# A four-layer graph network: its own order of work for the first and last three graphs, two layers in other layers' buffers, a new order for the graphs between

## The chip, the cores and the metric

The kernel runs on one core of one Trainium2 chip. The metric is the device time of one execution in microseconds (us); less is better. The core has TensorE (PE in the profile, its weight loads PEld), VectorE (DVE), ScalarE (ACT), GpSimd (POOL) and SyncE (SP), which run their own streams of instructions and wait for each other by semaphores.

## The reference

Thirty-two independent graphs, each with 512 nodes of 256 features (`x`) and a 512x512 adjacency matrix of 0 and 1 (`adj`). Each graph goes through four layers; every layer normalizes, takes the positive part, and adds its result to `x`:

```python
    h = jnp.maximum(_layernorm(x, axis=-1), 0.0)
    x = x + _L0_gnn_ref(h, adj, L0_gnn_W, L0_gnn_a_src, L0_gnn_a_dst)
    h = jnp.maximum(_layernorm(x, axis=-1), 0.0)
    x = x + _L1_gnn_ref(h, adj, L1_gnn_W, L1_gnn_a)
    h = jnp.maximum(_layernorm(x, axis=-1), 0.0)
    x = x + _L2_gnn_ref(h, adj, L2_gnn_a_0, L2_gnn_a_1, L2_gnn_a_2, L2_gnn_a_3)
    h = jnp.maximum(_layernorm(x, axis=-1), 0.0)
    x = x + _L3_gnn_ref(h, adj, L3_gnn_Wqkv, ...)
```

Layer 0 is graph attention with 4 heads: `Wh = h @ W`, scores from a sum of a source and a destination term, masked softmax, product with `Wh`, elu. Layer 1 is the same with one head and a softmax over the other axis. Layer 2 scores pairs of nodes by weighted inner products of `h`, softmax, product with `h`. Layer 3 is a transformer block with 8 heads of 32: qkv, masked softmax attention, output product, layer norm, two products with 1024 features between, layer norm.

## The kernel before

**The work of a graph.** `quick_path` writes every graph as 497 jobs, each for one engine (a job of PE is one to eight products of f32). I name a job by its number in the graph, `#0` to `#496`, which is its place in the table too:

| jobs | what |
|---|---|
| #0, #1 | loads of `adj` and `x` (SP) |
| #2 to #13 | masks `m`, `mT` (four transposing DMAs, #4 to #7) and `m3`; #3 checks `adj` |
| #14 to #42 | layer 0: norm, `h0`, its transposes on PE (#33 to #41) |
| #43 to #66 | layer 0: `wh` (PE #43 to #59), `ps_sp` (#63), and the trip of `rows` through DRAM (SP #65, #66) |
| #67 to #109 | layer 0: four heads (DVE `p`, PE `ps_o` #71 to #74, #81 to #84, #91 to #94, #101 to #104), elu and sum (#107 to #109) |
| #112 to #185 | layer 1: norm, transposes (#131 to #139), `wh` (#141 to #151), `ps_sp` (#156), trip of `rows` (#158, #159), `mc` and `p` (DVE #160 to #174), product `ps_o` (PE #176 to #182) |
| #189 to #264 | layer 2: norm, transposes (#208 to #216), scores (#220 to #252), product `ps_o` (PE #253 to #262) |
| #267 to #371 | layer 3: norm, transposes, qk and v, attention (`ps_s`, `ps_ct`, `ps_to`) |
| #373 to #414 | layer 3: `ps_wo` (#373 to #380), norm (#381 to #404), transposes `ps_t` (#405 to #412) |
| #417 to #496 | layer 3: `ps_f` (#417 to #438 and #441 to #473), last norm, store |

**The order.** Nothing is ordered by loops at run time. `Plan.put` (line 150) gives each job a place, `number * ROUND + table[at]` with ROUND = 100000 (line 153), and `carry_out` (line 178) emits all jobs of all graphs sorted by place, so each engine gets its stream in that order and works it off strictly in order. One table, `PLACES` (line 282), serves all 32 graphs. It runs from 0 to 491,710, so five graphs are in work at a time, one round apart.

**Buffers.** `K` (line 351) lists the kinds of buffers and their slots. Layer 0 has one slot each of `h0`, `h0T`, `wh0`, `rows0`, `e0`, and six of `p`. Layers 1 and 2 share `h1`, `h1T`, `wh1`, `p1`. Layer 3 has `h3`, `hT3`, `qk`, `vt`, `n` and two slots of `p3`. PSUM has two slots of `ps_a`, two of `ps_b`, and `ps_ct`, `ps_to`. A job that is first to use a slot waits for all users of the tile that was there.

**Constants.** The weights of layer 3 are loaded by POOL after the first `x` (line 795), and a few constants are formed at place 150000 (line 798), with one product `ps_bv`.

All of the jobs' instructions are made in `carry_out`, so the profile puts nearly all of DVE's and ACT's work at L214, PE's products at L259 and transposes at L257, DMAs at L235; tiles tell them apart.

Of the kernel before, what the change touches and what calls it, by code (L numbers as in the profile page):

```python
# [16 lines left out]
OP = mybir.AluOpType  # L17
AX = mybir.AxisListType

P = 128  # L20
# [102 lines left out]
class Plan:  # L123
# [6 lines left out]
        tensor_copy=(1,), tensor_scalar_max=(1,), tensor_scalar_mul=(1,),  # L130
    )

    def __init__(self, tc, table):
        self.tc, self.nc, self.table = tc, tc.nc, table
        self.jobs = []

    def graph(self, number):

# [11 lines left out]
    def put(self, engine, takes, ends, outs, ins, call, port=False, moves=None):  # L150

        j = Job()
        place = self.number * ROUND + self.table[self.at] if self.place is None else self.place
        j.place = (place, self.at)
        self.at += 1
        j.engine, j.takes, j.ends, j.call, j.port, j.moves = engine, takes, ends, call, port, moves
        j.after, j.homes = [], []
        before = set()
        for part, writes in [(p, True) for p in outs] + [(p, False) for p in ins]:
            h = part.home  # L160
            r0, r1 = int(part.rows.min()), int(part.rows.max())
            i0, i1 = int(part.index.min()), int(part.index.max())
            if in_psum(part):
                i0, i1 = 0, 1 << 20
            for k, w, a0, a1, b0, b1 in h.uses:
                if (w or writes) and k is not j and a0 <= r1 and r0 <= a1 and b0 <= i1 and i0 <= b1:
                    before.add(k)
            h.uses.append((j, writes, r0, r1, i0, i1))
            if h not in j.homes:
                j.homes.append(h)  # L170
                h.left += 1
        for k in before:
            assert k.place < j.place, "out of order"
            k.after.append(j)
        self.jobs.append(j)
        return j
# [61 lines left out]
    def load(self, tile, source, behind):  # L238
# [7 lines left out]

        return self.put("POOL", 1.0, 0.1, [], [], call)

    def matmuls(self, takes, *calls):

        real = lambda x: x.real() if isinstance(x, Part) else x

        def call():
            made = []
            for c in calls:
                if len(c) == 3:
                    made.append(self.nc.tensor.transpose(*map(real, c)))  # L257
                else:
                    made.append(self.nc.tensor.matmul(*map(real, c[:3]), start=c[3], stop=c[4]))  # L259
            return made  # L260

        outs = [c[0] for c in calls]
        ins = [x for c in calls for x in c[1:3] if isinstance(x, Part)]
        return self.put("PE", takes, takes + 0.2, outs, ins, call)
# [10 lines left out]
def width(args):  # L275
# [4 lines left out]

ROUND = 100000
PLACES = [
    19807, 0, 43241, 57619, 64598, 73580, 81389, 88138, 134062, 235662, 143142, 287307, 285553, 232853, 15635,
    15811, 28841, 27985, 23993, 15811, 30374, 30229, 32369, 32370, 32370, 32446, 32844, 48496, 34324, 44230,
    44177, 46695, 46041, 50344, 54161, 54792, 54792, 54792, 51041, 51777, 57310, 57310, 57310, 57738, 57738,
    57832, 57739, 58104, 61341, 61341, 67966, 61898, 61898, 67567, 69254, 72469, 69482, 77323, 74000, 76325,
    79818, 78024, 78024, 80713, 80713, 80714, 82170, 88138, 93984, 93675, 88138, 100363, 101562, 103520,
    103520, 103520, 103520, 99026, 98456, 107942, 108892, 114155, 115978, 115979, 116955, 117229, 118109,
    112967, 112266, 118498, 118106, 122333, 124077, 124856, 124856, 126720, 126720, 130323, 126361, 126793,
    124647, 132760, 132760, 132760, 132760, 134221, 134221, 134221, 134221, 134221, 134727, 134221, 156322,  # L290
    140191, 134912, 142057, 169073, 157725, 170057, 172384, 201862, 202787, 205641, 207797, 208539, 176096,
    208573, 211867, 216328, 218484, 218484, 219056, 219056, 219056, 219056, 219056, 218484, 218484, 218484,
    218484, 218485, 227052, 227119, 228253, 219613, 219613, 220424, 224906, 224906, 228631, 223683, 224122,
    224122, 229201, 229201, 232797, 231582, 232020, 232794, 233389, 243904, 244480, 249048, 254893, 242125,
    242231, 243790, 254173, 237217, 238008, 241105, 245079, 237839, 238826, 242604, 256707, 257566, 258334,
    259006, 259006, 259006, 259519, 259519, 259519, 259519, 259519, 392456, 255868, 267182, 259006, 259006,
    259892, 259665, 259006, 259006, 259892, 259665, 266786, 266786, 268621, 269711, 273176, 302934, 273176,
    273176, 273176, 277010, 277447, 281097, 281097, 281195, 281196, 281196, 281682, 281682, 281682, 281682,
    281683, 281196, 281683, 282840, 282840, 284327, 283254, 286775, 286821, 286821, 287236, 288036, 287335,
    282681, 282681, 283122, 282681, 284575, 293213, 293213, 295654, 291792, 291574, 293905, 297714, 297584,  # L300
    297714, 298819, 298819, 297714, 287489, 287489, 290592, 290231, 298206, 300033, 308229, 310297, 310297,
    303799, 303799, 303799, 305379, 305380, 306132, 308300, 312883, 316207, 394029, 437737, 327509, 328548,
    327753, 325228, 328998, 329876, 332238, 330645, 332238, 332502, 332502, 332608, 332717, 364575, 332717,
    332717, 332717, 332717, 332717, 338203, 340406, 340406, 340406, 340407, 340407, 340905, 341309, 341309,
    352943, 347109, 352371, 352371, 353369, 353369, 353417, 354661, 356381, 356381, 356381, 357144, 357399,
    346769, 348254, 348493, 351248, 352029, 352189, 352199, 352199, 352554, 359237, 359237, 359237, 359237,
    364034, 360298, 360301, 360448, 365688, 377452, 366095, 368722, 368232, 374829, 379739, 379671, 380891,
    379672, 382370, 383191, 386847, 392755, 392755, 387818, 392756, 395158, 396303, 407857, 382331, 382331,
    382615, 382634, 388690, 385894, 388773, 389314, 389314, 394131, 390806, 394842, 396200, 401293, 405927,
    398693, 403322, 398865, 403593, 407530, 409955, 410479, 412422, 412422, 408793, 409986, 423530, 354795,  # L310
    408893, 410479, 418263, 418263, 418263, 419191, 419191, 419191, 419191, 419128, 417119, 437177, 437347,
    419191, 420203, 420203, 420203, 420203, 420721, 420203, 420203, 421199, 422452, 422452, 423633, 423633,
    432009, 424134, 424134, 424718, 424718, 424759, 425616, 425916, 425916, 425916, 425916, 426698, 426841,
    426841, 426970, 427475, 430939, 430939, 427202, 428368, 428368, 428368, 429763, 429360, 431209, 431243,
    432263, 432263, 432291, 432540, 430070, 430071, 430071, 430071, 430446, 430071, 431829, 432836, 432836,
    435307, 436332, 440746, 435945, 435945, 436252, 436626, 436626, 437927, 444318, 444318, 444811, 444811,
    444811, 445291, 445291, 445291, 445291, 445447, 445572, 436110, 437653, 437653, 437653, 437653, 437653,
    438770, 440843, 440843, 440843, 440843, 440843, 440872, 442233, 442446, 442446, 442446, 445600, 445600,
    442446, 442446, 445601, 445601, 442446, 442704, 446845, 449648, 449758, 449759, 449759, 454221, 449777,
    450699, 450699, 450699, 450699, 450699, 450699, 491710,  # L320
]


# [1 line left out]
def quick_path(  # L325
# [35 lines left out]
    K |= {tag: Kind(dram, tag, 2) for tag in ("rows0d", "rows1d", "to_d", "in_d")}  # L361
    K |= {"ps_ct": Kind(psum, "ps_ct", 1), "ps_to": Kind(psum, "ps_to", 1)}
    K |= {"ps_a": Kind(psum, "ps_a", 2), "ps_b": Kind(psum, "ps_b", 2)}
    plan = Plan(tc, PLACES)

    def new(tag, name, shape, dtype=F32):
        return plan.tile(K[tag], name, shape, dtype)


    ident = const.tile([P, P], F32, name="ident")  # L370
# [295 lines left out]
    def layer3(b, x_t, m3):  # L666
# [29 lines left out]
        for g in range(KD):  # L696
            ps_ct = new("ps_ct", "ps_ct", [P, N])
            ps_to = new("ps_to", "ps_to", [P, N])
            for j in range(NT):
# [8 lines left out]
                        for r, at in enumerate(heads)  # L708
                    ),
                )  # L710
                p = new("p3", "p3", [P, HG, N])
                for q in range(HG // 2):
                    plan.act("activation", p[:, 2 * q : 2 * q + 2], ps[q], AF.Exp)
                plan.dve("tensor_mul", p, p, m3[:, j : j + 1].flat(lambda t: t.to_broadcast([P, HG, N])))
# [53 lines left out]
        for g in range(NF // 2):  # L768
            ps = new("ps_b", "ps_f1", [P, 2, N])
            if g % 2 == 0:  # L770
                f1 += [new("p3", f"f1_{b}", [P, HG, N])] * 4
            for q in (0, 1):
                f = 2 * g + q
                for k in range(KD):
                    plan.matmuls(FULL, (ps[:, q], ff1_t[:, k, cut(f, P)], tT[:, k], k == 0, k == KD - 1))
            for q in (0, 1):
                f = 2 * g + q
                plan.act("activation", f1[f][:, f % 4], ps[:, q], AF.Relu, bias=ff1b_c[:, f : f + 1], fixed=0.27)
# [13 lines left out]
        plan.dma(out[b].rearrange("(t p) d -> p t d", p=P), y, 1.75)  # L792


    plan.aside(max(PLACES[:2]) + 1)
    for tile_, source in late:
        plan.load(tile_, source, lambda: first)
    plan.aside(ROUND + ROUND // 2)
# [518 lines left out]
```

## Time and profile before

| | us |
|---|---|
| median of 3 runs (3751.09 to 3758.95) | 3752.26 |
| the profiled execution: its time | 3758.1 |
| the profiled execution: its span, first to last instruction | 3756.2 |

| | busy us | share of the span |
|---|---|---|
| PE | 3635.0 | 97% |
| PEld | 2366.4 | 63% |
| DVE | 2732.6 | 73% |
| ACT | 1803.8 | 48% |

The mean granted clock of TensorE is 0.976. The profiled execution's span is within 2 us of its own time, and its time is 5.8 us above the median. The page's slices are 94 us each; the start and the end of the span need finer windows.

### The profile page before, as it was taken

To read this page: it belongs to the slowest core of one execution; us is meant where nothing else is said; L and a number is where in the kernel's file an instruction comes from. 1 tells how busy PE (TensorE), PEld (TensorE's weight loads), DVE (VectorE), ACT (ScalarE), POOL (GpSimd) and SP (SyncE) were. 2 spreads that over 40 slices of the span, in tenths; PEclk is the share of its full clock that TensorE was granted. 3 is DMA by queue.
4 is the path that set the end of the run, shared out by engine and by line. 5 is a ranking of instruction groups with operands and counts; after the bars stand their busy time and mean duration, and the time that the engine had idled before them with its cause. 6 is when DMAs were issued, how large, how long until landed. Compare 5 with 4: busy or idle time off the path is not lost.

```text
span 3756.2 us, 51774 instructions
## 1 busy us (share of the span) xinstructions
PE 3635.0 (97%) x19974; PEld 2366.4 (63%) x19974; DVE 2732.6 (73%) x6267; ACT 1803.8 (48%) x3393; POOL 11.1 (0%) x25
## 2 busy tenths in 40 slices
PE   4799999999999999999999999999999999999996
PEld 4666766666766666666666666666666666666553
DVE  4577777877777777777787777787777777777653
ACT  1245445555444555444555544555544455544543
POOL 1000000000000000000000000000000000000000
PEclk7599999999999999999999999999999999999998
DMA  4111111111111111011111111111111111100000
GB/s 120 57 32 33 36 49 46 43 42 36 29 49 46 43 49 36 23 47 47 49 43 38 40 29 49 46 43 49 29 29 49 46 43 49 38 29 27 15 9 11
DMA packets 152349, 152.72 MB, mean 41 GB/s; under 512 B 87840, under 2 KB 122144, under 8 KB 148000
## 3 DMA queue, kind: packets, MB, share of 16 engines
q1 hardware_dynamic: 149632, 144.35, 13.8%
q0 software_dynamic: 1216, 3.94, 0.3%
q8 instruction: 159, 2.61, 0.3%
q10 hardware_dynamic: 1248, 1.05, 0.1%
q14 instruction: 94, 0.77, 0.1%
HBM read 114.57 MB, written 17.96 MB: 35 GB/s over the span
## 4 chain that ended last, share of the span: by engine, by line
PE 95%; DVE 3%; ACT 1%; DMA 1%; issue 1%; SPq 0%; ACTq 0%; DVEq 0%
PE ps_o L259 25%; PE ps_f L259 24%; PE ps_s L259 7%; PE ps_ct L259 7%; PE ps_wh L259 6%; PE ps_qk L259 6%; PE ps_to L259 6%; PE ps_e L259 4%; PE ps_t L257 4%; PE ps_v L259 3%; PE ps_wo L259 3%; DVE p L214 1%; PE ps_y L257 1%; DVE st L214 0%; DMA mT<-m 0%
## 5 line engine op out<-in xcount | busy, mean ns | idle before, releaser
L259 PE MATMUL ps_o<-wh,p 128*128 128x65 f32 (+1 forms) x5120 | 750.5, 303 | 30.2 <-DVE p L214 24.6
L259 PEld LDWEIGHTS ps_o<-wh,p 128*128 128x128 f32 x5120 | 705.6, 200 | 102.7 <-issue 60.5
L214 DVE TENSOR_TENSOR p<-p,m 128x2048 f32<-128x2048 f32 x256 | 582.7, 2286 | 29.7 <-ACT p L214 29.6
L214 ACT ACTIVATE p<-ps_s 128x1024 f32<-128x1024 f32 x512 | 501.2, 1022 | 208.1 <-PE ps_s L259 205.3
L259 PE MATMUL ps_f<-tT,ff_t 128*128 128x512 f32 x1024 | 462.7, 602 | 1.7 <-ACT tT L214 1.7
L259 PE MATMUL ps_f<-ff_t,f 128*128 128x256 f32 x2048 | 461.0, 379 | 0.0
L259 PEld LDWEIGHTS ps_f<-ff_t,f 128*128 128x128 f32 x2048 | 381.9, 190 | 64.0 <-issue 15.3
L214 DVE SCALAR_TENSOR_TENSOR p<-rows,rt,mT 128x512 f32<-128x512 f32 x512 | 370.1, 735 | 16.7 <-DMA mT<-m 16.7
L214 ACT ACTIVATE h<-x,shift,rstd 128x256 f32<-128x256 f32 x512 | 268.6, 595 | 152.8 <-PE ps_o L259 106.3
L259 PEld LDWEIGHTS ps_f<-tT,ff_t 128*128 128x128 f32 x1024 | 189.4, 192 | 229.3 <-issue 188.7
L259 PE MATMUL ps_s<-qk 32*128 32x512 f32 x2048 | 294.2, 640 | 1.3 <-ACT qk L214 0.8
L259 PE MATMUL ps_ct<-p,v 128*32 128x512 f32 x2048 | 272.0, 603 | 9.3 <-DVE p L214 6.3
L214 ACT ACTIVATE f<-ps_f,ff1b_c 128x512 f32<-128x512 f32 x256 | 164.8, 682 | 235.7 <-PE ps_f L259 235.7
L259 PE MATMUL ps_to<-p,ones 128*32 128x512 f32 x2048 | 266.6, 592 | 0.0
L259 PE MATMUL ps_qk<-h3T,wqkv_t 128*128 128x512 f32 x512 | 239.1, 594 | 0.0
L259 PE MATMUL ps_o<-h,p 128*128 128x257 f32 x1024 | 239.0, 385 | 0.0
L259 PEld LDWEIGHTS ps_o<-h,p 128*128 128x128 f32 x1024 | 190.1, 191 | 51.5 <-issue 26.0
L214 DVE BATCH_NORM_STATS2 st<-x 128x6 f32<-128x256 f32 x512 | 195.6, 415 | 6.8 <-DMA x<-in_x_dram 4.7
L214 ACT ACTIVATE rstd<-mv,eps 128x4 f32<-128x4 f32 x192 | 56.4, 294 | 298.6 <-DVE mv L214 286.0
L257 PE MATMUL ps_t<-ident,h 128*128 128x128 f32 x1024 | 172.6, 281 | 25.0 <-ACT h L214 17.6
L259 PEld LDWEIGHTS ps_s<-qk 32*128 32x128 f32 x2048 | 81.3, 182 | 164.6 <-ACT y L214 78.0
L257 PEld LDWEIGHTS ps_t<-ident,h 128*128 128x128 f32 x1024 | 130.8, 145 | 85.2 <-issue 52.3
(131 smaller groups left out, 4322.9 us busy)
## 6 DMA issues: line engine op xcount, KB each, us to landing
adj<-in_adj_dram SPq DMA_DIRECT2D x32, 1024.0 KB
rows<-rows_d SPq DMA_DIRECT2D x32, 1024.0 KB
x<-in_x_dram SPq DMA_DIRECT2D x32, 512.0 KB
rows<-rows_d SPq DMA_DIRECT2D x32, 512.0 KB
out_dram<-y SPq DMA_DIRECT2D x32, 512.0 KB
inv<-in_d SPq DMA_DIRECT2D x32, 256.0 KB
ff_t<-in_L_gnn_W_dram POOLq DMA_DIRECT2D x2, 1024.0 KB, 12.5
mT<-m SPq DMA_TRANSPOSE x128
```

Of the source, the lines that this page charges most:

```text
L214: return [getattr(unit, method)(*map(real, args), **{k: real(v) for k, v in kw.items()})]
L257: made.append(self.nc.tensor.transpose(*map(real, c)))
L259: made.append(self.nc.tensor.matmul(*map(real, c[:3]), start=c[3], stop=c[4]))
```

## The change

It does four things. A graph can have a table of its own (`own`), and the first three graphs (`FIRST`) and the last three (`LAST`) get one each. `PLACES` is replaced, for the 26 graphs between. In graph 1, the layer-0 tiles h0, h0T, wh0, rows0 and e0 lie in layer 3's buffers; in graph 31, layer 3's tiles lie in layer 0's buffers, and its `p3` and `f1` in `p1` and `adj`. A method `accumulate` is added that nothing calls. No job is added or removed: the 497 jobs of a graph, their operations and their sizes stay.

```diff
-    def __init__(self, tc, table):
-        self.tc, self.nc, self.table = tc, tc.nc, table
-        self.jobs = []
+    def __init__(self, tc, table, own=()):
+        self.tc, self.nc, self.table, self.own = tc, tc.nc, table, dict(own)
+        self.jobs, self.number = [], None
...
-        place = self.number * ROUND + self.table[self.at] if self.place is None else self.place
+        place = self.number * ROUND + self.own.get(self.number, self.table)[self.at] if self.place is None else self.place
...
 PLACES = [
-    19807, 0, 43241, 57619, 64598, 73580, 81389, 88138, 134062, 235662, 143142, 287307, 285553, 232853, 15635,
...
-    450699, 450699, 450699, 450699, 450699, 450699, 491710,
+    4941, 0, 45989, 55878, 52736, 53088, 65883, 75806, 126827, 257141, 153885, 318759, 211656, 217633, 19570,
...
+    442345, 444396, 453835, 453835, 478083,
+]
+
+FIRST = [
+    [
+        -232641, -430519, -208468, -143305, -187563, -187562, -126023, -120210, -1386, 231738, 69096, 52945,
...
-    plan = Plan(tc, PLACES)
+    own = {**dict(enumerate(FIRST)), **{B - len(LAST) + g: places for g, places in enumerate(LAST)}}
+    plan = Plan(tc, PLACES, own)
+
+    ELSEWHERE = {
+        1: dict(h0="n", h0T="hT3", wh0="p3", rows0="qk", e0="vt"),
+        B - 1: dict(h3="h0", hT3="h0T", qk="rows0", vt="e0", n="wh0"),
+    }
 
     def new(tag, name, shape, dtype=F32):
+        tag = ELSEWHERE.get(plan.number, {}).get(tag, tag)
         return plan.tile(K[tag], name, shape, dtype)
...
-                p = new("p3", "p3", [P, HG, N])
+                p = new("p3" if b < B - 1 else ("p1", "adj")[j % 2], "p3", [P, HG, N])
...
-                f1 += [new("p3", f"f1_{b}", [P, HG, N])] * 4
+                f1 += [new("p3" if b < B - 1 else ("p1", "adj")[g // 2], f"f1_{b}", [P, HG, N])] * 4
...
-    plan.aside(max(PLACES[:2]) + 1)
+    plan.aside(max(FIRST[0][:2]) + 1)
```

What the tables say is an order, which follows from sorting the places. PE's stream at the start, with g0 for graph 0 and the products' numbers:

| before | after |
|---|---|
| g0 #33 to #59, #63 | g0 #33 to #59, #63 |
| g0 heads #71 to #94 | g0 heads #71 to #94 |
| g0 head #101 to #104 | g1 transposes, with g0 #101 to #104 between |
| `ps_bv` | g1 `wh` #43 to #49, `ps_bv`, g1 `wh` #53 to #59 |
| g1 transposes, `wh`, #63 | g1 #63 |
| g1 #71 to #84 | g1 #71 to #74, half of g0 layer-1 transposes, g1 #81, other half, #82 to #84 |
| g0 layer-1 transposes, `wh` with g1 #91 to #94 between | g0 layer-1 `wh`, #156 |
| g0 #156, g1 #101 to #104 | g1 #91 to #94, g2 transposes, two `wh`, g1 #101 to #104 |
| g2 transposes, g0 #176 to #182 with g2 `wh` between | g0 #176 to #182, six `wh` of g2 |

On SP, the four `mT` transposes of a graph stood on both sides of `rows_d` and `rows` (#65, #6, #66, #7); for g0 and g1 they now all stand ahead of #65. `x` of g1 is loaded right after `adj` of g0, `x` of g2 after `rows` of g0. On DVE, g0's `mc` and `p` of layer 1 (#160 to #174) stood behind g1's elu (#108, #109); most of them now stand ahead of g1's last head. At the end, PE had g31 #253 to #262 in two parts ahead of g30 `ps_wo` and then g30 #405; now g30 `ps_wo` comes first, then three of the four `ps_o` of g31, then g30 #405. From g31's attention on, PE's order is the old one, up to two products of the last `ps_f`.

## Prediction

> **What bounds the kernel now.** I read three views in this order: busy time in windows (columns: the window, its length, then PE, PEld, DVE, ACT, POOL busy with counts, PE's granted clock, DMA share, GB/s), the chain that ended last, and the timeline of the two ends.
>
> ```profile
> 25.00:75.00 50.00, 28.80 (x128) 27.75 (x128) 20.37 (x47) 2.72 (x6) 0.00 (x0) 0.54 0.21 63
> 75.00:125.00 50.00, 33.49 (x135) 28.96 (x135) 18.45 (x48) 8.29 (x22) 0.00 (x0) 0.60 0.21 64
> 125.00:175.00 50.00, 33.66 (x119) 26.32 (x119) 26.27 (x77) 14.41 (x37) 0.00 (x0) 0.60 0.12 33
> 600.00:1600.00 1000.00, 1000.00 (x5601) 650.55 (x5603) 762.42 (x1750) 504.14 (x952) 0.00 (x0) 1.00 0.15 41
> 3600.00:3625.00 25.00, 19.10 (x86) 11.15 (x85) 18.36 (x42) 4.78 (x10) 0.00 (x0) 0.83 0.02 5
> 3675.00:3757.00 82.00, 52.47 (x250) 26.96 (x250) 31.48 (x54) 22.98 (x35) 0.00 (x0) 0.87 0.04 11
> ```
>
> In the middle PE has no idle time and the full clock; no other engine is over 0.77 busy. At the start PE is idle a third of the time and runs at about half its clock. The chain of waits gives the middle's pace:
>
> ```profile
> 303.75 8.84 PE ps_f L259 x20
> 415.13 8.84 PE ps_f L259 x20
> 526.51 8.85 PE ps_f L259 x20
> ```
>
> One graph each 111.38 us, and 32 of them are 3564 us. The span is 3756.2, so 192 us lie outside. To place them I use the first arguments of `matmuls` as the measure of PE work (108.5 us a graph; 111.38 were measured, a factor of 1.026). At 247.1 us PE has begun products with 107.4 us of work ahead of them: 110.2 at the middle's pace, so the start costs **137 us**; the end costs **about 53** and the rest nothing. Only these ends can give much. What they consist of is in PE's timeline (start, us, instruction, idle before it and who ended it):
>
> ```profile
> 34.78 0.66 PE L259 MATMUL ps_o<-wh,p 128*128 128x65 f32 x2 [9.96 <-DVE p L214]
> 36.68 7.52 PE L259 MATMUL ps_o<-wh,p 128*128 128x65 f32 x34 [1.24 <-DVE p L214]
> 62.22 7.06 PE L259 MATMUL ps_o<-wh,p 128*128 128x65 f32 x32 [2.86 <-DVE mv L214]
> 76.55 2.04 PE L259 MATMUL ps_bv<-wo_t,bv_w 128*128 128x256 f32 x4 [7.28 <-issue]
> 95.96 0.66 PE L259 MATMUL ps_o<-wh,p 128*128 128x65 f32 x2 [8.89 <-DVE p L214]
> ...
> 144.11 1.11 PE L257 MATMUL ps_t<-ident,h 128*128 128x128 f32 x4 [5.71 <-DVE mc L214]
> 148.04 1.11 PE L257 MATMUL ps_t<-ident,h 128*128 128x128 f32 x4 [2.82 <-ACT h L214]
> ...
> 3617.57 2.17 PE L257 MATMUL ps_t<-ident,n 128*128 128x128 f32 x8 [5.03 <-ACT n L214]
> 3707.73 2.16 PE L257 MATMUL ps_t<-ident,n 128*128 128x128 f32 x8 [5.03 <-ACT n L214]
> ```
>
> A head's 32 records take 7.1 us in the start. The idle time is graph 0's and graph 1's trips of `rows` (10 and 9 us), graph 0's elu (7), graph 0's layer 1 around 144 us (11 in three pieces), and two norms at the end (5 each).
>
> **What the Trainium skill says.** "Trainium Kernel Development and Optimization", Performance Expectations: matmul busy time is a bad metric since matmuls are pipelined; here it reads 97% while 192 us lie outside the pace, so I don't use it. "TensorE: Matmul & The Clock Gate", part 1 (What's actually happening): the array starts throttled to half its clock, and about 3.4 us of sustained activity releases it. The trace agrees on the two levels (0.50 and 1.00 in windows of 4 us) but not on the release: heads ran 7 us without a gap at 0.50, so heads alone don't warm it. "DMA: Bandwidth & Descriptors" (Two DMAs through the same engine are not ordered): a reader of what another DMA writes must wait for its semaphore; so SP stands still between `rows_d` and `rows`, which took 1.23 us where nothing stood between (132.03 to 133.26).
>
> **The start, step by step.**
> - *Graph 0 up to its heads.* All four `mT` go ahead of `rows_d`. The first `p` waited for the last one, issued at 28.34; it will wait for `rows`, at most 1 to 2 us less. `x` of graph 1 (512 KB) now stands behind `adj` while the DMAs are full (share 0.96 to 1.22): at 382 GB/s up to 1.4 us more. I take 0, bounds -2 and +1.4.
> - *Graph 0's heads* (34.8 to 69.3 us). DVE now does graph 1's `m` (1.22) and `m3` (1.22) between `p`s, so head 1 starts some 2 us later; graph 1's transposes (8 of 0.21) fill the 2.86 before the last head. I take 0, bounds -2 and +3.
> - *Graph 1's layer 0.* Before, its `h0` waited for graph 0's elu (buffer `h0`), and 26.7 us passed from the last head (69.3) to its first (95.96). Now transposes are done by then. What is left: 8 `wh` of 0.9 cold (half before `ps_bv`), `ps_bv`, whose `bv_w` is on DVE behind graph 0's elu (ends near 75), so at about 77; then the other `wh`, `ps_sp` near 82. Then `rows`: 0.3 (spr) + 1.4 + landing. Packets of layer 1's 512 KB ended 3 us after issue; 1 MB gets 4 to 5. First `p` near 88 to 89 in place of 95.06: **-6**. `ps_bv` limits it now. If it came free at once, it would be -9.
> - *Graph 0's layer 1.* DVE stood in order: at 138.44 it turned to graph 1's elu, and `mc` came at 143.43 although `rows` had been issued at 133.26. Now `mc` and `p` (4 x 0.68, 4 x 0.83, small ones) lie under graph 1's last two heads (2 x 7 us cold). From the end of the last head to `ps_o` of layer 1 were 13.5 us (138.4 to 151.9), with only 2 us of transposes; the transposes now come before. So **-11**, and bounds -13 (all) and -6 (if `rows` or `p` is late, as DVE also has graph 1's `p`).
> - *Up to saturation* (161 to 230 us) the order is nearly the same, layer 2 of graph 0 still being a chain of its own; **-1**, bounds -4 and +2. A warm clock is not in the sum: if layer 1's `wh`, now contiguous (3.45 us of work, 7 cold), releases it, the two heads and transposes behind it (about 8.7 us of work) take that much less: up to -8.
>
> Sum of the start: **-18**, bounds -28 and -8.
>
> **The end.** Graph 30's `ps_wo` now has 5.4 us of graph 31's `ps_o` behind it. From the last `ps_ct` (3605.4) to the norm's `ps_t` (3617.6) were 12.2 us with 7.1 of work. After: DVE's two halves of 1/sum (1.76 + 0.42 each) hold `ps_wo` about 1 us, then all is covered; 10.9 of work in about 11.8, so -4. The clock fell in that gap (0.83), and 13.7 us of `ps_f` took 16.9: another -3. Graph 29's same norm had 2.4 us of idle, half of it covered: -1. For graph 31 nothing covers its norm (5.03), attention (some 10 us of gaps) and tail from 3740.8 on, and the order is the old one; the new buffers take waits away that PE doesn't feel there. Sum **-8**, bounds -10 and -3.
>
> **The middle.** PE is full, so only small losses can change. 108.5 against 111.38 is spread over hundreds of jobs; the largest single loss, `ps_wh` to `ps_f` #417, is 0.16. A PE job that needs a new wait on another engine cost 0.034 on average, any other 0.011. Sorting the new table gives 63 such jobs a graph, 65 before: -0.05 us a graph. Following each wait back by data alone with the trace's durations, the tightest has 0.53 us to spare (0.19 before), and 25 have under 2 us (31 before). So **0** over some 27 graphs, bounds -0.3 and +0.4 a graph: -8 and +11.
>
> **Sum.** -18 - 8 + 0 = -26. The profiled execution's own time of 3758.1 would be 3732; the median of the runs, 5.8 lower, becomes **3726 us**.
>
> **Rivals.**
> 1. *The clock warms in the start too* (-8), and the middle gains 0.2 us a graph (-5): 3713. For: at 156 us dense `ps_o` of layer 1 went from 0.60 to 1.00 within 4 us. Against: at 116 to 131 us `wh` mixed with heads stayed at 0.50.
> 2. *The start's gain is given back before saturation*: layer 2 and 3 of graph 0 wait for DVE, now with more of graph 1's and 2's work ahead. Then the end's 8 remain and a little: 3742. Against: DVE is busy 0.4 to 0.6 there.
> 3. *The middle gets slower.* In the old order 11.2 us of PE work lie between layer 1's `ps_sp` and the first `mc` on DVE; in the new one 4.1, and the trip takes 0.3 + 1.2 + 3.2 = 4.7. DVE would stand in front of it with everything queued behind: graph 13's and 15's `p`, norms, whose users on PE have as little as 0.5 us to spare. Graph 1's elu (1.06 ACT, 2 x 1.23 DVE) stands ahead of it and should cover it. It decides above 1 us a graph (26 / 27); at 1.5 it gives 3726 + 41 = 3767.
> 4. *A place is wrong* (a buffer taken too early, a constant used before it is formed): I found graph 0's first `ps_qk` at 326134 behind the constants at 150000; this has no chance worth a number.
>
> **How the numbers follow.** Forecast 0.60 (own range 3709 to 3744), warm start 0.15, given back 0.10, slower middle 0.15. A measurement of this kernel tells 0.2% (7.5 us) from no change. Faster: 0.60 + 0.15 and a third of case 2, less 0.02 of the forecast's upper end: 0.76. Same: 0.09. Slower: 0.15. The range must reach past case 2 but not to case 3: **3704 to 3750**; it leaves out 0.15 above and some 0.04 below.
>
> **What would show it.** Right: graph 1's first head near 89 us, layer 1's `ps_o` within 2 us of graph 1's last head and near 135, no idle above 1 us before `ps_t` near the last-but-one norm, the pace still 111.4. Wrong: a pace above 112, idle time of DVE ended by the DMA `rows` in the middle, or PE not full by 215 us.

## The result, and the profile after

The changed kernel takes 3743.20 us in the median of 12 runs (3737.76 to 3745.93), the kernel before 3755.12 (3750.60 to 3760.10); the ratio is 0.9966, interval [0.9958, 0.9975]. It is faster, by 12 us, inside the predicted range of 3704 to 3750, but by less than half of the 26 us that the prediction worked out. The profiled execution took 3737.76 us with a span of 3735.4, which is 20.8 less than that of before. That is more than the medians differ, and the reason is at the end of this section.

Busy time in windows, changed kernel (columns as in the prediction's first view):

```profile
75.00:125.00 50.00, 35.84 (x150) 29.64 (x149) 26.07 (x68) 8.77 (x27) 0.00 (x0) 0.60 0.21 64
125.00:175.00 50.00, 41.22 (x188) 33.57 (x188) 33.97 (x95) 15.83 (x36) 0.00 (x0) 0.82 0.16 53
175.00:225.00 50.00, 45.83 (x264) 30.72 (x263) 33.59 (x85) 27.25 (x57) 0.00 (x0) 1.00 0.07 19
225.00:275.00 50.00, 47.43 (x323) 29.82 (x320) 43.72 (x86) 20.90 (x36) 0.00 (x0) 1.00 0.21 62
600.00:1600.00 1000.00, 999.79 (x5618) 653.10 (x5617) 767.91 (x1760) 509.37 (x954) 0.00 (x0) 1.00 0.15 42
2600.00:3400.00 800.00, 793.42 (x4453) 519.94 (x4452) 609.69 (x1398) 398.88 (x748) 0.00 (x0) 1.00 0.15 40
3600.00:3625.00 25.00, 24.08 (x85) 14.70 (x85) 6.42 (x26) 10.60 (x19) 0.00 (x0) 1.00 0.01 2
```

and two of the same windows in the kernel before, which the prediction doesn't show:

```profile
225.00:275.00 50.00, 50.00 (x291) 25.89 (x289) 41.63 (x86) 33.12 (x60) 0.00 (x0) 0.98 0.14 39
2600.00:3400.00 800.00, 800.00 (x4513) 517.62 (x4516) 614.63 (x1402) 404.33 (x761) 0.00 (x0) 1.00 0.16 43
```

Up to 225 us PE has more to do, and from 125 us on a higher clock (0.82 and 1.00 where 0.60 and 0.81 stood). But at 225 to 275, where PE was full before, it is not, and from 2600 to 3400, where it was full too, 6.6 us are idle. The chain of waits gives the pace of the middle, by the same instructions in three graphs running:

```profile
732.22 12.07 PE ps_f L267 x28
...
843.28 12.07 PE ps_f L267 x28
...
954.57 12.07 PE ps_f L267 x28
```

The first step is 111.06 us, against 111.38 before; the second is 111.29, with one small stand-still in it. PE's timeline of the ends:

```profile
74.80 1.73 PE L267 MATMUL ps_bv<-wo_t,bv_w 128*128 128x256 f32 x4 [2.41 <-ACT rt L214]
89.20 1.35 PE L267 MATMUL ps_o<-wh,p 128*128 128x65 f32 x4 [6.87 <-DVE p L214]
...
112.39 3.68 PE L267 MATMUL ps_o<-wh,p 128*128 128x65 f32 x32
119.77 2.17 PE L265 MATMUL ps_t<-ident,h 128*128 128x128 f32 x8 [3.69 <-ACT h L214]
...
143.63 1.94 PE L265 MATMUL ps_t<-ident,h 128*128 128x128 f32 x8 [1.44 <-DVE spr L214]
...
3601.61 8.85 PE L267 MATMUL ps_f<-tT,ff_t 128*128 128x512 f32 x20 [0.87 <-ACT tT L214]
...
3689.26 2.16 PE L265 MATMUL ps_t<-ident,n 128*128 128x128 f32 x8 [5.02 <-ACT n L214]
```

Graph 1's first head starts at 89.20 (95.96 before). Of the 5.71 and 2.82 us before graph 2's transposes, in graph 0's layer 1, 3.69 are left (119.77). Of the two norms that cost 5 us each at the end only graph 31's is left (3689.26).

To see where the time went, I put the two kernels beside each other by PE work done (the sum of the first arguments of `matmuls`). Of each kernel there are two traces, since both were run once more; in each kernel the two part before 230 us and run nearly in step from there, 4.7 us apart (between 4.7 and 6.1 in the changed kernel). Compared are the earlier with the earlier and the later with the later; the table gives changed minus before, in us. The first row depends on this choice of pairs (-31.1 and -21.5 in the other one); what is won or lost behind it does not, within 1 us.

| PE work done | time before | later pair | earlier pair |
|---|---|---|---|
| 90 (start over) | 229 | -26.2 | -26.4 |
| 500 | 650 | -13.3 | -13.9 |
| 2900 | 3113 | -19.8 | -20.7 |
| 3200 | 3422 | -10.4 | -11.8 |
| all | 3741 | -13.8 | -13.8 |

So by the earlier pair the start wins 26.4, **12.5 are given back between 229 and 650 us**, the middle wins 6.8, **8.9 are lost between 3113 and 3422**, and the end wins 2.0. The two losses lie where a table of its own meets the table of the middle: I call them the first and the second joint. The profiled pair of the prediction was a later execution of before and an earlier one of the changed kernel: 13.8 and 4.7 make 18.5 by PE's last product, and the rest of the 20.8 lies behind it, where the changed kernel took 13.2 us to its end and the one before 15.4. The two pairs are two executions of each kernel; the medians of the runs differ by 12.

The waits of PE in the first joint (198 to 560 us; columns: who waits for whom, us in total, times, the longest), the six largest of twelve:

```profile
PE ps_t L265 <- DVE spr L214: 1.3, 2, 0.9
PE ps_wo L267 <- DVE cT L214: 1.2, 1, 1.2
PE ps_qk L267 <- ACT v L214: 0.9, 1, 0.9
PE ps_wh L267 <- DVE h0T L214: 0.9, 2, 0.5
PE ps_e L267 <- ACT h2T L214: 0.8, 1, 0.8
PE ps_ct L267 <- DVE p L214: 0.7, 1, 0.7
```

and the four largest in the second (3000 to 3450 us):

```profile
PE ps_t L265 <- DVE wh L214: 1.8, 1, 1.8
PE ps_sp L265 <- ACT rt L214: 1.2, 1, 1.2
PE ps_wh L267 <- DVE h1T L214: 1.0, 2, 0.7
PE ps_t L265 <- DVE o L214: 0.5, 1, 0.5
```

In the kernel before PE has no wait from 228 to 3450 us. No single wait is large; there are many, ended by VectorE and by ScalarE, in 8.6 and 6.6 us of idle time in all (9.4 and 7.1 in the second trace).

### The profile page after: what moved, and what is told of

Read it like the earlier page. It is cut to its first block, busy times and chain, and to the rows that moved or that the text cites. A ratio compares the mean times of both kernels' runs of the same rounds, so it can differ in the third digit from the quotient of the medians.

```text
span 3735.4 us, 51907 instructions
## 1 busy us (share of the span) xinstructions
PE 3624.7 (97%) x19974; PEld 2360.3 (63%) x19974; DVE 2741.7 (73%) x6267; ACT 1811.3 (48%) x3393; POOL 11.1 (0%) x25
## 4 chain that ended last, share of the span: by engine, by line
PE 92%; DVE 4%; ACT 2%; DMA 1%; issue 1%; ACTq 0%; SPq 0%; DVEq 0%
PE ps_o L267 24%; PE ps_f L267 24%; PE ps_s L267 7%; PE ps_wh L267 6%; PE ps_ct L267 6%; PE ps_qk L267 6%; PE ps_to L267 5%; PE ps_t L265 4%; PE ps_e L267 4%; PE ps_wo L267 3%; PE ps_v L267 3%; DVE p L214 2%; PE ps_y L265 1%; DMA rows<-rows_d 1%; ACT p L214 1%
## 5 line engine op out<-in xcount | busy, mean ns | idle before, releaser
L267 PE MATMUL ps_o<-wh,p 128*128 128x65 f32 (+1 forms) x5120 | 738.9, 301 | 22.1 <-DVE p L214 19.9
L267 PEld LDWEIGHTS ps_o<-wh,p 128*128 128x128 f32 x5120 | 693.0, 198 | 92.6 <-issue 46.4
L267 PEld LDWEIGHTS ps_o<-h,p 128*128 128x128 f32 x1024 | 189.9, 191 | 53.2 <-issue 26.4
L214 DVE BATCH_NORM_STATS2 st<-x 128x6 f32<-128x256 f32 x512 | 204.2, 415 | 8.8 <-DMA x<-in_x_dram 4.8
L214 DVE TENSOR_TENSOR u<-ps_f,n 128x512 f32<-128x512 f32 x64 | 44.3, 692 | 220.0 <-PE ps_f L267 220.0
L265 PEld LDWEIGHTS ps_t<-ident,h 128*128 128x128 f32 x1024 | 122.3, 144 | 92.3 <-issue 50.6
## 6 DMA issues: line engine op xcount, KB each, us to landing
ff_t<-in_L_gnn_W_dram POOLq DMA_DIRECT2D x2, 1024.0 KB, 14.4
```

What stands on the lines that cost most here:

```text
L214: return [getattr(unit, method)(*map(real, args), **{k: real(v) for k, v in kw.items()})]
```

## The experiments

Two questions: what are the parts worth, each alone, and why do the joints lose. In these runs the kernel before took 3752.9, 3758.7 and 3758.0 us in the median (one set for each of the three groups). Its times fall in two groups, near 3751 and near 3759, between which its median jumps; so the ratio to it, with its 95% interval, is given too. Leads "by work" are again those in PE's work done.

**The new table alone.**

```
-    own = {**dict(enumerate(FIRST)), **{B - len(LAST) + g: ... LAST ...}}
+    own = {}
-    plan.aside(max(FIRST[0][:2]) + 1)
+    plan.aside(max(PLACES[:2]) + 1)
```

> The new table for all 32 graphs, no tables of their own for the first and last three and no buffers elsewhere. In the changed kernel's trace the middle's pace was 111.06 us a graph against 111.38, which over some 22 graphs is 7 us. Theory S (parts add up; own tables gain at the start and lose at the two places where they join the middle's table): the pace is 111.06 over 26 or more graphs, PE stands still nowhere between 300 and 3400 us for more than 0.5 us at a time, and the time is 7 to 11 us under the kernel before, as its start and end are those of before give or take 3. Rival R (the new pace comes from the buffers that the own tables leave free, or is paid back elsewhere): the pace is 111.4, or the time is within 3 us of before.

The edit as run left `ELSEWHERE` in place, other than the text above says; the same holds for the next two kernels. Measured: 3740.15 us, ratio 0.9960 [0.9947, 0.9972]. Theory S was right in the pace (111.06), and PE has no wait between 214 and 533 us. It was wrong in the size, in the start, which wins 14 us by 230 us without any own table, and in that PE would nowhere stand still for more than 0.5 us: three waits before `ps_y` take 2.4 us up to 3450 us, the longest 1.4. So all of the change's gain is there with neither `FIRST` nor `LAST`.

**Without the last three graphs' table.**

```
+    own = dict(enumerate(FIRST))
```

> The changed kernel without the last three graphs' own table and without graph 31's buffers elsewhere: the new table runs through to graph 31. Theory S: between 3000 and 3450 us the changed kernel lost about 9 us on PE (stand-still before transposes, wh and ps_sp) where graphs 26 to 30 meet the own table; that loss goes, and so do the gains of the end (about 2 net, 7 gross); so this is 2 to 9 us faster than the changed kernel, about 3736 in the median. Rival R (the pipe runs empty there whatever the table, because no graph 32 follows, or the own table at the end is worth more than it loses): the loss of 9 stays, or the end loses more than that, and the time is the changed kernel's or up to 8 longer, 3743 to 3751.

Measured: 3743.50 us, 0.9971 [0.9961, 0.9981]; the changed kernel had 0.9966. By time, nothing changed, and neither theory is told apart. By the trace, both are half right: PE has no wait at all between 3000 and 3450 us, and the lead over before, which falls by 8.9 or 9.4 us between work 2900 and 3200 in the changed kernel, grows by 0.7 here. So the loss of the second joint belongs to the own table and not to the pipe running empty. Yet from work 2900 on this kernel loses 4.8 us to its end against before, where the changed one loses 6.9 in its earlier trace and 6.0 in its later one; the own table costs 1 to 2 net, too little for the times to tell.

**Without the first three graphs' table.**

```
+    own = {B - len(LAST) + g: places for g, places in enumerate(LAST)}
+    plan.aside(max(PLACES[:2]) + 1)
```

> The changed kernel without the first three graphs' own table and without graph 1's buffers elsewhere: the new table from graph 0 on. In the changed kernel's trace PE was 30 us ahead of before at the same work by 230 us, and 19 ahead by 500 us. Theory S: the 11 us that were given back belong to the joint between graph 2's table and graph 3's, so they don't occur here; the start is as long as before give or take 4, and the time is 19 us over the changed kernel's profiled execution, 3755 to 3764. Rival R (the new table gives part of the start's gain by itself): under 3752. Rival S2 (the give-back comes from the new table starting up in any case): over 3765.

Measured: 3737.88 us, 0.9957 [0.9944, 0.9971]. Theory S failed by 19 us, and rival R holds: `FIRST` can be left out without any loss. By work 90 it is 15.3 us ahead of before, and up to the second joint it gives nothing back (16.4 at work 500, 22.0 at 2900); at that joint it loses 8.4.

**The kernel before once more.** The same file.

> The kernel before, once more, for a second trace. Its 12 times fall in two groups, 3750.6 to 3752.8 and 3757.4 to 3760.1; the profiled one belongs to the upper group. Theory C (the groups differ by when the TensorE clock is released in the first 200 us): if this execution falls in the lower group, its windows up to 225 us show the same gaps and a higher granted clock in one of them, and beyond 250 us the two traces run in step. Rival (a DMA or DVE stand-still somewhere in the middle that comes and goes): the traces part between 250 and 3700 us.

Measured: 3755.42 us, 1.0003 [0.9995, 1.0011]. Its profiled execution fell in the lower group (span 3751.4). It is 4.7 us ahead of the first trace at work 90 and 4.8 at the end: theory C. To work 90 PE stands idle for 79.8 us here and for 78.7 in the first trace, but is busy for 144.7 against 150.5 with the same work: the gain is the clock, which is at 1.00 through the middle from 191 us on here and from 227 on there. The rival is out.

**The changed kernel once more.** The same file.

> The changed kernel once more, for a second trace. Its 12 times lie between 3737.8 and 3745.9, and the profiled one was the lowest. Theory C (executions differ by when the TensorE clock is released before 230 us, as the two traces of the kernel before did, which part by 4.7 us between 90 and 230 us and run in step from there): this execution, if it is a longer one, is behind the first trace by 3 to 8 us of which all lies before 230 us, with a lower granted clock in the windows of 125 to 225 us; after that the two stay within 1 us. Rival (short stand-stills that come and go in the middle, such as one of 0.6 and one of 1.4 us before ps_y in the run of the middle table alone): the traces part after 500 us by more than 2 us.

Measured: 3744.75 us, 0.9969 [0.9960, 0.9978]. Span 3741.3. It is behind the first trace by 4.9 us at work 90, by 5.6 at work 2900, 6.1 at 3000 and 4.7 at the end: theory C again, but with 1.2 us of wandering in the middle where at most 1 was expected. To work 90 idle time is the same (59.6 and 59.4 us), busy time is not (143.4 and 138.6). The clock shows it; windows of 4 us of the first trace, and then of this one:

```profile
124.00:128.00 4.00, 4.00 (x27) 3.90 (x25) 2.80 (x9) 1.37 (x5) 0.00 (x0) 0.71 0.03 6
128.00:132.00 4.00, 4.00 (x25) 3.62 (x24) 1.79 (x3) 1.65 (x3) 0.00 (x0) 1.00 0.00 0
132.00:136.00 4.00, 4.00 (x20) 3.51 (x19) 3.83 (x8) 0.60 (x1) 0.00 (x0) 1.00 0.00 0
```

```profile
124.00:128.00 4.00, 4.00 (x15) 3.59 (x16) 2.82 (x6) 0.25 (x2) 0.00 (x0) 0.50 0.03 6
128.00:132.00 4.00, 4.00 (x21) 4.00 (x21) 1.14 (x7) 1.71 (x4) 0.00 (x0) 0.50 0.00 0
132.00:136.00 4.00, 4.00 (x15) 3.42 (x15) 2.06 (x4) 1.06 (x1) 0.00 (x0) 0.64 0.00 0
```

PE is full in all six; the full clock comes some 8 us later in the second (column before the last two), and graph 0's first `ps_o` of layer 1 starts at 132.5 in place of 128.9 us.

**The new table alone, with no buffers elsewhere.** As the first experiment, and

```
-        1: dict(h0="n", h0T="hT3", wh0="p3", rows0="qk", e0="vt"),
-        B - 1: dict(h3="h0", hT3="h0T", qk="rows0", vt="e0", n="wh0"),
```

> The new table for all 32 graphs, no tables of their own, and, other than in middle_only, whose edit left the second graph's and the last graph's buffers elsewhere in place, no buffers elsewhere either. Middle_only was 10 us ahead of the second trace of before by 230 us. Theory T (that comes from the new table's order alone): same as middle_only, 3736 to 3742, and 8 to 11 us ahead at 230 us. Rival E (it comes from graph 1's buffers elsewhere, which let its h0 go ahead of graph 0's elu): the lead at 230 us goes, and the time is about 3750.

Measured: 3739.93 us, 0.9957 [0.9943, 0.9970], and 14.4 us ahead of the second trace of before by work 90 (the 10 in the text above were read against the wrong one of the two traces: middle_only belongs to the first, where it is 14.3 ahead). Theory T: neither the buffers nor the own tables are needed for the gain. To work 90 its PE is idle for 73.9 us and busy for 136.2 (79.8 and 144.7 in that trace of before): the larger part of the 14.4 is a higher clock. Its windows:

```profile
225.00:275.00 50.00, 50.00 (x345) 28.06 (x344) 46.27 (x86) 25.91 (x46) 0.00 (x0) 1.00 0.20 63
600.00:1600.00 1000.00, 998.83 (x5615) 652.24 (x5614) 766.96 (x1753) 509.54 (x954) 0.00 (x0) 1.00 0.15 41
2600.00:3400.00 800.00, 798.81 (x4511) 526.89 (x4510) 614.10 (x1416) 404.97 (x763) 0.00 (x0) 1.00 0.15 40
```

PE is full at 225 to 275 us, with DVE busier (46.27) than in the changed kernel's first joint (43.72).

**The first joint in another order.** A replay of the changed kernel's trace (each job with its measured duration, engines in order, data and buffers as in the plan) has 11.3 us of PE's idle time between 195 us and 560 where 8.6 were measured. Moving jobs in it until the idle time was gone gave an order, which was written into the tables of graphs 0 to 7:

```
+OWN = {
+    0: [
...
     own = {**dict(enumerate(FIRST)), ...}
+    own |= OWN
```

> The changed kernel with the jobs of graphs 0 to 7 in another order from 195 us on (148 of PE's jobs and 397 of DVE's stand elsewhere), found by replaying the trace's own durations and moving jobs until PE's stand-stills there were gone. Nothing else is changed, and the work is the same. Theory J (the 12 us given back between 200 and 530 us are a matter of order where graph 2's own table meets the middle's): PE's idle time between 198 and 560 us falls from 8.5 us to under 2, and the time falls by 6 to 11 us, to about 3734. Rival D (PE was ahead of what VectorE can supply there, and would stand still in any order): idle time of PE stays above 5 us, or turns up behind 560 us, and the time is within 3 us of the changed kernel's.

Measured: 3736.78 us, 0.9953 [0.9940, 0.9967]; the changed kernel beside it 0.9969. PE's idle time from 198 to 560 us is 1.8 us. The time falls by 8, as theory J says. By work the joint is mended only in part: between work 90 and 500 the lead over before still falls by 7 us (12.5 in the changed kernel), of which under 2 are idle time; what the rest is stays open.

**Both joints in another order.** As the last one, and with tables in `OWN` for graphs 25 to 31 too, up to the very end.

> As joint_in, and in the same way also the jobs of graphs 25 to 31 from 3040 us on in another order (340 of PE's jobs and 851 of DVE's in all). Theory J, for the other joint (graphs 26 to 30, where the changed kernel gave back 9 us): by the replay another 13 us less, of which some 8 before 3450 us and 5 in the last 150; with the replay's own error (2.8 us too many of stand-still in the first joint) I expect 8 to 13, so about 3723. Rival D (with no graph 32 there is too little other work to put under the waits): less than 4 us below joint_in.

Measured: 3729.82 us, 0.9932 [0.9918, 0.9945], 7 us below joint_in: short of the 8 to 13 that were expected, and against rival D. Idle time of PE from 3000 to 3450 us: 2.7 us, after 6.6. But the joint is not where most of it is won. By its trace, of its fastest execution (3724.13), it is 30.8 us ahead of the second trace of before at the end, where the changed kernel's first is 13.8 ahead; of these 17 us it has 5.0 by work 2900 (first joint), wins 2.8 between 2900 and 3200 (second joint), and 9.2 behind that, 7 of them between 3420 and 3450. So the new order helped the last graphs' end more than the second joint.

**Only 36 jobs moved.** The replay was asked for as few moves as possible. Of the 36, 11 are PE's, 16 VectorE's and 9 ScalarE's; most move by one to twelve places:

```
+MOVED = {
+    (0, 315): (355878, 4.0), (0, 347): (375342, 347.0), (0, 353): (381348, 352.0),
...
-        j.place = (place, self.at)
+        j.place = MOVED.get((self.number, self.at), (place, self.at)) if self.place is None else (place, self.at)
```

> The changed kernel with 36 of its 15,926 jobs moved (graphs 0 to 5, most by under 20 places in the order; 10 on PE, the rest on VectorE and ScalarE), which the replay of the trace names as enough: it takes 10.2 us off the first joint. Theory J: what the first joint costs are a few jobs that stand in front of, or behind, those of the neighbouring graph's table; PE's idle time between 198 and 560 us falls from 8.5 to 10 us to under 3, and the time falls by 6 to 9, to about 3736 beside some 3744 for the changed kernel. Rival D2 (the joint is mended only by a new order as a whole, as joint_in has it): idle stays above 5, the time within 3 us of the changed kernel's.

Measured: 3733.76 us, 0.9939 [0.9928, 0.9951]. Idle time of PE from 198 to 560 us: 2.0 us. Between work 90 and 500 the lead over before falls by 3.2 us, where it fell by 12.5 in the changed kernel. So most of what the first joint cost was the place of a few jobs. All of PE's waits there:

```profile
PE ps_qk L267 <- ACT h3T L214: 1.2, 1, 1.2
PE ps_t L265 <- DVE spr L214: 0.5, 1, 0.5
PE ps_wh L267 <- ACT h1T L214: 0.2, 1, 0.2
```

How one of them went. In the changed kernel (timeline, all engines):

```profile
230.09 1.02 ACT L214 ACTIVATE p<-ps_s 128x1024 f32<-128x1024 f32 x1 [2.83 <-issue]
231.01 0.58 ACT L214 COPY h2T<-ps_t 128x512 f32<-128x512 f32 x1
...
231.64 1.12 PE L267 MATMUL ps_e<-h2T,ha 128*128 128x512 f32 x2 [0.83 <-ACT h2T L214]
```

Graph 1's `h2T`, a copy of 0.58 us whose input PE had finished by 227.1, stood on ACT behind graph 0's `p`, and ACT stood still for 2.83 us until PE had made the scores for that `p`. Only then came the copy, and PE stood before `ps_e` for 0.83. With the jobs moved, that `p` stands behind the copy:

```profile
230.60 1.07 PE L265 MATMUL ps_t<-ident,h 128*128 128x128 f32 x8 [0.48 <-DVE spr L214]
...
231.77 0.59 ACT L214 COPY h2T<-ps_t 128x512 f32<-128x512 f32 x1
...
234.52 3.27 PE L267 MATMUL ps_e<-h2T,ha 128*128 128x384 f32 x8
...
234.68 1.94 ACT L214 ACTIVATE p<-ps_s 128x1024 f32<-128x1024 f32 x2 [2.32 <-issue]
```

The copy runs as soon as the transposes are done, 2.75 us before the first `ps_e`, and PE has no idle time among its four products. PE's own order is the same here in both kernels.

**The 36 jobs moved, and no table for the last three.**

> The same 36 jobs moved, and neither the last three graphs' own table nor graph 31's buffers elsewhere: the new table runs through to the end. Parts add up: the start is 12 us better than that of the new table alone (middle_plain, about 3740), with the joint mended it keeps 8 to 10 of it, and the end is that of middle_plain, so 3730 to 3733, 2 to 5 under joint_few. Rival (the own table of the end is worth having once the rest is mended): at or above joint_few.

Measured: 3731.62 us, 0.9937 [0.9925, 0.9950]. That is within what was expected: by work the first joint mended is worth 9 to the changed kernel, and the table at the end costs 2 net. By the times alone this can't be told from joint_few.

## Why the prediction was half right

*The start, -18 in the prediction: -26.4 by 229 us, and then 12.5 of it lost.* Its pieces held, and for PE's idle time the sum was nearly right: to work 90 (earlier pair) PE stands idle for 59.4 us in place of 79.8, 20.4 less. The other 6 us are busy time, 138.6 in place of 144.7 with the same work. Graph 0's heads: 35.5 to 69.1 us, nothing gained. Graph 1's layer 0: -6 was said, the first head came 6.8 earlier; `ps_bv` did stand at the limit (74.80, with 2.41 idle before it), and `ps_sp` at 81.94, for which 82 was said. Graph 0's layer 1: its first `ps_o` was to come within 2 us of graph 1's last head and near 135; it came with it, at 128.9. That is 23 us earlier than in the first trace of before and 20 earlier than in the second, where 17 were summed. The excess fits the clock, which the text named (up to -8) and left out of the sum: windows of 4 us show full clock at 112 to 116 and 128 to 140 us, where the first trace of before had 0.50, and graph 1's third head (112.39) takes 3.68 us for its 32 records where a head took 7.1.

*The first joint: the missing term, and the step that failed.* "Up to saturation the order is nearly the same" was carried on as if, with PE full, the start's lead were kept to the end; "the middle" then priced the new table for some 27 graphs by its steady state alone, at 0. The joints between the tables so stood at nothing, without a reason. But in graphs 1 to 4 the order is a mixture: jobs of `FIRST` and of the new table, each fitted to neighbours of its own kind. What was priced by sorting the table was never priced there. It costs 12.5 us: 8.6 of it are PE's idle time between 198 and 560 us; the rest is spread too thinly to name. The sign "PE not full by 215 us" came: at 225 to 275 us 2.6 us of PE are idle. Rival 2, the start's gain given back, had the right idea, the wrong place (before saturation, where the gain held) and too narrow a cause (DVE's load: middle_plain keeps PE full with a busier DVE, and ScalarE ends about half of the waits).

*What follows for `FIRST`.* It wins 12 us over the new table alone by 229 us (26.4 against 14.4) and pays 12.5 at its joint. The prediction put the whole start on it. The new table, run from graph 0 on, wins 14 there by itself, 5.9 of idle time and 8.5 of busy time, which the text didn't ask about; why its order goes with a higher clock was not tried.

*The middle, 0 in the prediction: -6.8.* Waiting jobs were priced at 0.034 us each on average, so that 65 to 63 gave -0.05 a graph. The trace shows that the average is made of two values. Over graphs 8 to 21, a job's loss being how much later it starts than the shortest time from the job before it, in either kernel, allows, 55 of the 65 waiting jobs of before lose nothing and the other ten 0.05 to 0.16 us each, 1.04 in all; of the 63 after, 56 lose nothing and seven 0.63. Jobs without a new wait went from 0.65 to 0.73, and some of these, nine in each kernel, lose 0.05 to 0.10 as well. The sum is -0.32 a graph, just past the lower bound of -0.3. The count of waits said nothing of it; which jobs lose goes with the order, and what makes them lose, a wait or something else, was not tried and stays open. Rival 3's wait, `mc` on DVE for `rows`, is there once in the steady stretch, for 0.5 us, and twice at the second joint, for 4.2 (at 3199 and 3299); PE goes on for more than 35 us after each of these two before it next stands still.

*The end, -8 in the prediction: -2.0, and 8.9 lost ahead of it.* The steps that were priced came: between work 3370 and 3390, graph 30's `ps_wo`, its norm and its `ps_f`, the lead grew by 7.7 us, where 4 + 3 were said, and the clock stayed at 1.00 (3600 to 3625 us). The rest did not: the 2.3 us before that place and the 3.4 after it, in the two last graphs' attention, are lost again, and the second joint was no term of the sum at all. From work 2900 on the four kernels without `LAST` lose 2.6 to 5.2 us of their lead, those with it and its joint unmended 4.6 to 6.9; kernels that differ in little else lie 1 to 3 apart, which is what `LAST` costs.

*The buffers elsewhere* were of no use by themselves: the new table does as well without them. Whether `FIRST` and `LAST` could do without them was not run. Rival 4, a wrong place, did not come.

In sum: -26.4 + 12.5 - 6.8 + 8.9 - 2.0 = -13.8, against -18 + 0 - 8 = -26. The two joints, 21.4 us, are what the prediction lacked, and the end won 6.0 less than it said. The start won 8.4 more, most of it the clock, and the middle 6.8 more, which made up 15 of these 27. The range had room for these two, the sum had neither; without them the change would have come to about +1 us. That the time still fell inside the range is luck.

Two sums of the prediction are off by little: 137 and 53 us make 190 where 192 were to be placed, and the bounds of the start's pieces add up to -30 and about -6, not -28 and -8. Neither bears on the result.

## What to carry to other kernels

Where an order is written out per stage, price the seams between the stages as stages of their own: a full PE on both sides says nothing of the graphs in which two orders mix. A replay of a trace with measured durations, in-order engines and the true dependencies can do this: here, made from the changed kernel's own trace, it put the idle time of the first joint at 11.3 us where 8.6 were measured, and found the 36 moves that mend most of it. Whether a replay from the trace of before would have shown the joint ahead of the run was not tried. Idle time alone is not the measure: joint_in had next to none there and still lost 7 us by work. And before a part of a change is credited with a gain, ask what the rest of the change does without it.

## What the runs showed of the hardware

In the first 230 us the TensorE clock comes in spells: in the changed kernel's first trace windows of 4 us show 1.00 at 112, 128 to 140, 152 and from 168 us on, and 0.50 or a mixture between them, with PE full in several of the slow ones. Between 109 and 167 us the stretches at one clock are 10.2, 6.8, 17.1, 6.8, 6.8 and 10.2 us long, all multiples of 3.4. In the second trace of the same kernel the spells lie elsewhere, and the two executions end 4.7 us (by PE's work) apart; the same 4.7 part the two traces of the kernel before. So a single profiled pair could have shown anything between 9 and 19 us of PE's time where 13.8 is right. In the middle of the kernel before, PE started without delay at 55 of 65 places where it had a new semaphore wait to check, and 0.05 to 0.16 us late at ten, the same ones in each graph; as jobs without such a wait are late by 0.05 to 0.10 at nine places, this is not shown to be the price of a wait.
